# A GNN's matrix of edge counts: products of one-hots on TensorE in place of one scatter per 128 edges

## The chip, the cores and the metric

The kernel runs on one core of one Trainium2 chip. The metric is the device time of one execution in microseconds (us). Engines are named as in the profile: PE (TensorE; PEld is its weight load), DVE (VectorE), ACT (ScalarE), POOL (GpSimd) and SP (SyncE, which here only issues DMAs).

## What is computed

A graph of 6250 nodes with 128 features each and 106250 edges, sorted by destination, 17 edges a node on the mean; each node has an edge to itself. Four blocks follow one another, each as `x = layernorm(x + block(x))`:

```python
def sage(h, Wl, bl, Wr):            # block 0: two of these, with relu between
    agg = segment_sum(h[src], dst) / maximum(segment_sum(1, dst), 1)[:, None]
    return agg @ Wl.T + bl + h @ Wr.T

def gcn(x, W, b):                   # block 1: one, then relu and @ W_lin; block 2: two
    deg = segment_sum(1, dst + loops); dinv = rsqrt(deg)
    return segment_sum((x @ W)[src] * (dinv[src] * dinv[dst])[:, None], dst + loops) + b

deg = segment_sum(edge_weight, dst); dinv = where(deg > 0, rsqrt(deg), 0)   # block 3
w = dinv[src] * edge_weight * dinv[dst]
for l in range(3):                  # nine hops in all
    out = h @ W[l, 0]; x = h
    for k in range(1, 4):
        x = segment_sum(w[:, None] * x[src], dst); out = out + x @ W[l, k]
    h = relu(layernorm(h + out + bias[l]) * gamma[l] + beta[l])
```

All sums over edges are sums with the same 6250 x 6250 matrix: its entry is the number of edges from a source to a destination (blocks 0 to 2), or the sum of their weights (block 3).

## The kernel before

**Tiling.** Nodes are padded to 49 windows of 128 (`NW`). Destinations are taken in 13 chunks `c` (`NC`) of three or four windows (`SHAPE`, first window `START[c]`, width 384 or 512 columns). A product of one chunk is, for each source window `s`, a 128 x 128 table (features of 128 sources) times a 128 x 512 block of the matrix, summed in PSUM over the 49 windows `s`.

**The matrices in DRAM.** `counts` holds bytes (39 MB), `weights` holds f32 for the first eight chunks (`ND`; 100 MB). Cell (source, destination) lies in chunk order, then by source in its window (partition), source window and destination. `empty` (L203) fills them with zeros on SP's queue. The edges are cut into 49 blocks (`NB`) of 128 rows of 17 edges (`KD`). For each block

- `fetch` (L642 to L644) loads the rows' keys (destination and source in one number), records and weights by three DMAs on SP,
- `cell` (L650 to L704) works on DVE: it compares each edge with the 48 neighbours (`J`) before and behind it, so that equal edges are counted once, and makes the cell's address `celli`, its count `cval` and its weight `wval`,
- `scatter` (L575) issues 17 indirect DMAs on POOL, each writing 128 cells. All of them stand in one order, `queue`/`in_line`.

**Stage 1** is the first layer of block 0, for c = 0 to 12. `fetch_chunk(c + 2)`, a fill of `counts`, and `count_cells(c + 1)` come first, then `degrees` for the blocks of the chunk: 17 one-hots of the destinations on DVE (L718) and 17 products on PE (L719), so that the in-degree and the sum of weights come out for each node, copied by ACT (L721) and turned by PE (L724); `norms` makes the scale factors. Then `counted_sum` (from L466): every seven windows `columns` (L454) loads 448 KB of `counts` into one of seven buffers `slots`, once every scatter of the chunk's blocks is done; ACT casts two windows at a time from byte to fp32r (L488, three buffers `wides`), and PE multiplies (L495) with the high and the low half of the table, `t0hi` and `t0lo`. Where the second layer's table `t1` of the windows below `START[c]` is already there, the same cast serves a second sum, "half", which goes to DRAM (`halves`). After the sum ACT copies it out (L509), PE multiplies with the layer's weights (L428), DVE adds. After chunks 7 to 10 two "early" sums each (e = 0 to 7) take the second layer's windows from `START[e]` to 31 (`KNOWN`). A fill of 12.5 MB of `weights` is issued after each of chunks 0 to 7.

**Stage 2** is the rest of blocks 0 to 2, with the same `counted_sum`; casts alternate between DVE (`widev`) and ACT (`wides`). Beside it POOL scatters `wval` into `weights` (33 blocks, 561 DMAs), released in groups behind products by `Paced`.

**Stage 3**, the nine hops, multiplies by `weights` for the first eight chunks (L1217, loads by `columns`) and by edges gathered with indirect DMAs for the rest (L1133, L1186).

**Setup** before stage 1 loads the edges, writes `keys`, `recs` and `edges` to DRAM, checks on the chip whether the input fits this way (else `general_way` runs), and branches.

The order on each engine is the order in which the program issues (the framework adds the semaphores), so a cast, a copy or a scatter waits for all that its engine was given before it.

Of the kernel before, what the change touches and what calls it, by code (L numbers as in the profile page):

```python
# [47 lines left out]
P = 128  # L48
N = 6250
# [35 lines left out]

SLOTS, LOADS, STEP, HOTS, GROUP = 30, 12, 2, 5, 4
# [43 lines left out]
def load_weights(nc, a, const, work, ps, ident, tags):  # L130
# [18 lines left out]
    transposed("w1l", a["L0_gnn_W1l"])  # L149
    transposed("w1r", a["L0_gnn_W1r"])  # L150
    transposed("w2l", a["L0_gnn_W2l"])
    transposed("w2r", a["L0_gnn_W2r"])
    bcast("b1l", a["L0_gnn_b1l"], D)
    bcast("b2l", a["L0_gnn_b2l"], D)
# [22 lines left out]
def kernel(ctx: ExitStack, tc: tile.TileContext, a: dict, out: bass.AP):  # L177
# [15 lines left out]
    counts = dram.tile([BASE[NC] + 4 * NB * KD * P, 1], U8, name="counts")  # L193
# [6 lines left out]
    def empty(mats, dt, c, engine):  # L200
        n = 7 * width(c) // (4 if dt == U8 else 16)
        z = zeros[:].bitcast(dt)[:, :n]
        ins = fills[dt, c] = engine.dma_start(  # L203
            mats[BASE[c]:BASE[c + 1]].rearrange("(p s f) o -> p s (f o)", p=P, f=n),
            z.unsqueeze(1).to_broadcast([P, NW * width(c) // n, n])).ins
        tc.declare_no_dep(ins, group=f"cells {dt}", reason="another chunk")
        tc.add_to_no_dep_group(f"cells {dt}", ins)
        return ins

    with tc.tile_pool(name="setup", bufs=1) as setup, \  # L210
            tc.tile_pool(name="ps_setup", bufs=2, space=PSUM) as ps:

        def spread(name, ap, dt):
            t = setup.tile([P, L + 2 * J], dt, name=name)
            nc.sync.dma_start(t[:], bass.AP(ap.tensor, ap.offset, [[L, P], [1, L + 2 * J]]))
            return t
# [4 lines left out]
        dsti = spread("dsti", a["dst"], I32)  # L221
# [3 lines left out]
        main = slice(J, J + L)  # L225


# [3 lines left out]
        nc.vector.tensor_scalar(k1[:], dsti[:], 1023, 13, op0=ALU.bitwise_and, op1=ALU.logical_shift_left)  # L231
        nc.vector.tensor_scalar(k2[:], dsti[:], 20, 23, op0=ALU.logical_shift_right, op1=ALU.logical_shift_left)
# [5 lines left out]
        nc.sync.dma_start(keys[J:].rearrange("(p e) o -> p (e o)", p=P), key[:, main])  # L238


        def field(at):
# [18 lines left out]
        empty(counts, U8, 0, nc.sync)  # L260

# [7 lines left out]
        dst = setup.tile([P, L + 2 * J], F32, name="dst")  # L269
# [6 lines left out]
        nc.vector.tensor_sub(t1[:], dst[:, 2 * J:2 * J + L], dst[:, main])  # L276
        nc.vector.tensor_scalar(t2[:], dst[:, main], float(NOWHERE), None, op0=ALU.is_lt)
        nc.vector.scalar_tensor_tensor(t2[:], t1[:], 0.0, t2[:], op0=ALU.is_equal, op1=ALU.mult)
        nc.vector.tensor_reduce(odd[:, 1:2], t2[:], AX.X, ALU.max)
        nc.vector.tensor_scalar(t2[:], t1[:], float(NOWHERE // 2), None, op0=ALU.is_lt)  # L280
        nc.vector.scalar_tensor_tensor(t2[:], t1[:], 1024.0, t2[:], op0=ALU.is_ge, op1=ALU.mult)
        nc.vector.tensor_reduce(odd[:, 2:3], t2[:], AX.X, ALU.max)
# [3 lines left out]
        dmax = setup.tile([P, RPP], F32, name="dmax")  # L286
        nc.vector.tensor_reduce(dmin[:], by_row(dst[:, main]), AX.X, ALU.min)
        nc.vector.tensor_reduce(dmax[:], by_row(dst[:, main]), AX.X, ALU.max)
        rowi = setup.tile([P, RPP], I32, name="rowi")
        nc.gpsimd.iota(rowi[:], pattern=[[1, RPP]], base=0, channel_multiplier=RPP)  # L290
        nc.vector.tensor_scalar(rowi[:], rowi[:], ~(P - 1), None, op0=ALU.bitwise_and)
        even = setup.tile([P, RPP], F32, name="even")
        nc.vector.tensor_copy(even[:], rowi[:])
        d1 = setup.tile([P, RPP], F32, name="d1")
        d2 = setup.tile([P, RPP], F32, name="d2")
        nc.vector.tensor_sub(d1[:], dmax[:], even[:])
        nc.vector.tensor_scalar(d1[:], d1[:], float(2 * P), None, op0=ALU.is_ge)
# [3 lines left out]
        nc.vector.tensor_sub(d2[:], dmin[:], even[:])  # L301
        nc.vector.tensor_scalar(d2[:], d2[:], -float(P), None, op0=ALU.is_lt)
# [6 lines left out]
        row = setup.tile([P, RPP], F32, name="row")  # L309
        nc.gpsimd.iota(row[:], pattern=[[1, RPP]], base=1, channel_multiplier=RPP,  # L310
                       allow_small_or_imprecise_dtypes=True)
# [43 lines left out]
    with tc.If(go == 1) as fork:  # L355
        usual_way(tc, a, out, dram, ident, part, first, over, keys, recs, edges, counts, weights, fills, empty)
# [5 lines left out]
def usual_way(ctx, tc, a, out, dram, ident, part, first, over, keys, recs, edges, counts, weights, fills, empty):  # L362
# [9 lines left out]
    iota = const.tile([P, NEAR * P], F16, name="iota")  # L372
    nc.gpsimd.iota(iota[:], pattern=[[1, NEAR * P]], base=0, channel_multiplier=0,
# [12 lines left out]
    stacked = early.tile([P, DH], F32, name="stacked")  # L386
    nc.vector.tensor_add(stacked[:], ident[:, :DH], ident[:, DH:])
    wt = load_weights(nc, a, early, work, ps, ident, ("y", "pp"))
# [63 lines left out]
    def columns(t, c, mat, dt, step, s0):  # L452
        cw, s1 = width(c), min(s0 + step, NW)
        load = nc.sync.dma_start(t[:, :(s1 - s0) * cw], mat[BASE[c]:BASE[c + 1]].rearrange(  # L454
            "(p f) o -> p (f o)", p=P)[:, s0 * cw:s1 * cw]).ins
        needs = [ins for i in blocks_near(c) for ins in scattered[dt, i]]
        tc.declare_no_dep(load, group=f"cells {dt}", keep=needs, reason="others' cells")
        tc.add_to_no_dep_group(f"cells {dt}", load)
        for ins in needs:
            tc.add_manual_dep(load, ins.name, SYNC, reason="the matrix is complete")  # L460
        return t
# [4 lines left out]
    def counted_sum(pool, c, parts, turns, own=False, wide_bufs=3, slots=None, since=0, until=NW, also=None):  # L466
# [5 lines left out]
        for s in range(since, until):  # L472
            r = (s - since) % step
            if r == 0:
                t = next(slots) if slots is not None else pool.tile([P, step * CW], U8, name="cols", tag="cols")
                t = columns(t, c, counts, U8, min(step, until - s), s)
                if own:
                    for j, w in enumerate(windows_of(c)):
                        if s <= w < min(s + step, until):
                            loop = t[:, (w - s) * cw + j * P:(w - s) * cw + (j + 1) * P]  # L480
                            nc.vector.tensor_tensor(loop, loop, ident8[:], op=ALU.add)
            if not todo:
# [5 lines left out]
                copy(wide[:, :n * cw], t[:, r * cw:(r + n) * cw])  # L488
                todo = [wide[:, i * cw:(i + 1) * cw] for i in range(n)]
            cols = todo.pop(0)  # L490
            for into, of_block, begin, end in [(acc, parts, since, until)] + ([also] if also else []):
                if s < end:
                    lhss = of_block(s)
                    for i, lhs in enumerate(lhss):
                        product = nc.tensor.matmul(into[:, :cw], lhs, cols, start=s == begin and i == 0,  # L495
                                                   stop=s == end - 1 and i == len(lhss) - 1).ins
                paced.product(product, len(lhss))
# [16 lines left out]
    kept = ctx.enter_context(tc.tile_pool(name="kept", bufs=1))  # L514
# [53 lines left out]
    def scatter(mat, dt, vals, i):  # L568

        group = f"cells {dt}"  # L570
        needs = [fills[dt, c] for c in chunks_near(i) if (dt, c) in fills]
        mine = scattered[dt, i] = []
        bounds = {} if dt == U8 else {"bounds_check": mat.shape[0] - 1, "oob_is_err": False}
        for k in range(KD):
            ins = nc.gpsimd.indirect_dma_start(  # L575
                out=mat[:], out_offset=bass.IndirectOffsetOnAxis(ap=celli[:, i, k:k + 1], axis=0),
                in_=vals[:, i, k:k + 1], in_offset=None, **bounds).ins
            tc.declare_no_dep(ins, group=group, keep=needs, reason="no cell is written twice")
            tc.add_to_no_dep_group(group, ins)
            for need in needs:  # L580
                tc.add_manual_dep(ins, need.name, SYNC, reason="empty")
            if dt == F32:
                tc.add_manual_dep(ins, last_count.name, ORDER, reason="needed later")
            mine.append(in_line(ins))
            yield ins
        queue.append(mine[-1])

    class Paced:

        PRODUCTS, GROUP, FIRST = 3.4, 8, 80  # L590

        def __init__(self, todo):
            self.todo, self.products, self.begun = todo, 0, 0
            self.some(self.FIRST)

        def some(self, n, behind=None):
            for i in range(n):
                ins = next(self.todo, None) if self.todo else None
                if ins is not None and i == 0 and behind is not None:
                    tc.add_manual_dep(ins, behind.name, SYNC, reason="the products go ahead")  # L600

        def product(self, ins, n):
            self.products += n
            if self.todo and self.products >= self.begun * self.PRODUCTS:
                self.begun += self.GROUP
                self.some(self.GROUP, ins)

        def rest(self):
            self.some(len(dense) * KD)
            self.todo = None  # L610

    paced = Paced(None)
# [977 lines left out]
```

## Time and profile before

| | us |
|---|---|
| median of 3 runs (lowest, highest) | 5808.2 (5804.29, 5808.4) |
| the profiled execution, its own time | 5803.66 |
| its span, first to last instruction | 5801.9 |
| PE busy in the span | 5259.3 (91%) |
| POOL busy | 4159.0 (72%) |
| DVE busy | 3122.8 (54%) |
| ACT busy | 2152.6 (37%) |
| first product of stage 1 (L495) | 165.5 |
| last product of stage 1 | 1194.4 |
| first product of stage 2 | 1203.0 |
| last product of stage 2 | 2152.4 |

The mean granted clock of TensorE over the span is 0.965 of full speed. A group's line in the profile reads: line, engine, operation, output<-inputs, shapes, number; busy us and the mean ns of one; then the idle time of the engine just before these instructions and what ended most of it. "issue" means that the engine waited for nothing that the profile shows. A line of the slices has 40 digits, each the busy share of 1/40 of the span in tenths. A line of the waits reads: engine and line, what it waited for, us in total, times, longest us.

### The profile page before, as it was taken

What the parts mean: (1) busy time and instruction counts of PE and PEld (TensorE: products, weight loads), DVE (VectorE), ACT (ScalarE), POOL (GpSimd) and SP (SyncE); (2) the same over time, 40 slices, a digit from 0 to 9 for tenths busy, and PEclk for the clock granted to TensorE, in tenths of its full rate; (3) what the DMA queues carried; (4) which work ended last, traced back from release to release, by engine and by line L of the source; (5) the groups of instructions that cost most, each with busy time, mean ns of one, the idle gap of its engine ahead of it and who ended that gap; (6) DMA issues with size and microseconds to landing.
All of it is one profiled execution on the core that took longest, in us unless ns stands there. A gap on an engine that the chain in (4) does not pass through costs nothing. (4 is left out here: it accounts for less than half of the span.)

```text
span 5801.9 us, 70518 instructions
## 1 busy us (share of the span) xinstructions
PE 5259.3 (91%) x19429; PEld 3137.9 (54%) x19429; DVE 3122.8 (54%) x8865; ACT 2152.6 (37%) x4470; POOL 4159.0 (72%) x4206
## 2 busy tenths in 40 slices
PE   0657579799999999999999999999999999999997
PEld 0334457476788775555555555555455555555453
DVE  7685455258855664434446644444456544444566
ACT  1323356347655443323333323323333333333333
POOL 5777777778877417767767767767777677777776
PEclk9878799899999999999999999999999999999997
DMA  5768783146544459999999999999999999999995
GB/s 183 235 196 253 217 252 94 59 141 180 153 133 136 147 166 332 324 316 323 324 318 314 309 316 324 324 316 323 304 316 310 299 323 323 318 323 323 315 332 171
DMA packets 686931, 1503.75 MB, mean 259 GB/s; under 512 B 152167, under 2 KB 338427, under 8 KB 686267
## 3 DMA queue, kind: packets, MB, share of 16 engines
q1 hardware_dynamic: 503618, 1256.33, 64.1%
q0 software_dynamic: 134144, 182.36, 11.7%
q10 hardware_dynamic: 48760, 60.45, 3.1%
q8 instruction: 154, 2.52, 0.2%
q14 instruction: 255, 2.08, 0.1%
HBM read 1309.15 MB, written 189.54 MB: 258 GB/s over the span
## 5 line engine op out<-in xcount | busy, mean ns | idle before, releaser
L1217 PE MATMUL acc<-weighed,hop 128*128 128x512 f32 x7056 | 3380.4, 594 | 13.9 <-DMA weighed<-weights 7.5
L1133 POOL DMA_INDIRECT rows<-stored,gsrc x2763 | 2651.0, 959 | 993.6 <-issue 383.6
L1186 PE MATMUL gacc<-both,oh 128*128 128x256 f32 x2754 | 1779.0, 655 | 34.7 <-DVE both L1170 34.6
L1169 ACT ACTIVATE both<-rows,gwgt 128x128 fp32r<-128x128 f32 x2754 | 1059.7, 399 | 1979.2 <-DMA rows<-stored,gsrc 1766.8
L1217 PEld LDWEIGHTS acc<-weighed,hop 128*128 128x128 f32 x7056 | 1152.3, 190 | 938.8 <-issue 832.9
L1170 DVE SCALAR_TENSOR_TENSOR both<-rows,gwgt,both 128x128 fp32r<-128x128 f32 x2754 | 931.3, 349 | 1311.3 <-ACT both L1169 1302.2
L495 PE MATMUL acc<-wides,t 128*128 128x512 f32 (+1 forms) x3083 | 875.6, 394 | 358.3 <-ACT wides L488 237.4
L575 POOL DMA_INDIRECT counts<-cval,celli x833 | 826.3, 992 | 265.0 <-issue 243.8
L1186 PEld LDWEIGHTS gacc<-both,oh 128*128 128x128 f32 x2754 | 525.1, 191 | 691.5 <-issue 382.1
L495 PEld LDWEIGHTS acc<-wides,t 128*128 128x128 f32 x3083 | 568.3, 191 | 496.0 <-ACT wides L488 262.9
L575 POOL DMA_INDIRECT weights<-wval,celli x561 | 643.3, 1147 | 171.0 <-issue 155.5
L488 ACT CAST wides<-slots 128x1024 fp32r<-128x1024 uint8 (+3 forms) x684 | 562.5, 862 | 522.6 <-DMA slots<-counts 305.8
L1149 DVE TENSOR_TENSOR oh<-places,gdst 128x640 fp32r<-128x640 f32 x612 | 479.2, 783 | 236.3 <-PE gacc L1186 235.6
L495 PE MATMUL acc<-widev,t 128*128 128x512 f32 (+1 forms) x2044 | 575.6, 390 | 16.1 <-DVE widev L488 11.6
L495 PEld LDWEIGHTS acc<-widev,t 128*128 128x128 f32 x2044 | 376.3, 189 | 97.1 <-DVE widev L488 27.6
L718 DVE TENSOR_SCALAR oh<-iota,dloc 128x384 bf16<-128x384 f16 x833 | 215.7, 321 | 360.9 <-PE pd L719 360.7
L488 ACT CAST wides<-cols 128x1024 fp32r<-128x1024 uint8 (+1 forms) x364 | 284.7, 797 | 283.6 <-DMA cols<-counts 152.2
L488 DVE CAST widev<-cols 128x1024 fp32r<-128x1024 uint8 (+1 forms) x364 | 247.3, 684 | 175.1 <-PE acc L495 139.7
L495 PE MATMUL half<-wides,t 128*128 128x512 f32 (+1 forms) x606 | 188.3, 389 | 0.0
L719 PE MATMUL pd<-oh,lw 128*4 128x384 bf16 x833 | 176.8, 339 | 9.5 <-DVE oh L718 7.6
L488 DVE CAST widev<-slots 128x1024 fp32r<-128x1024 uint8 (+3 forms) x239 | 157.4, 676 | 17.1 <-PE acc L495 13.4
L1052 DVE TENSOR_TENSOR y<-pp,dinvw 128x256 f32<-128x256 f32 (+2 forms) x153 | 82.4, 539 | 150.1 <-PE pp L428 149.7
(266 smaller groups left out, 2792.9 us busy)
## 6 DMA issues: line engine op xcount, KB each, us to landing
weighed<-weights SPq DMA_DIRECT2D x1728, 512.0 KB
weights<-zeros SPq DMA_DIRECT2D x8, 12544.0 KB
slots<-counts SPq DMA_DIRECT2D x174, 448.0 KB
cols<-counts SPq DMA_DIRECT2D x140, 448.0 KB
rows<-stored,gsrc POOLq DMA_INDIRECT x2763
counts<-zeros SPq DMA_DIRECT2D x10, 3136.0 KB
stored<-hop ACTq DMA_DIRECT2D x74, 256.0 KB
weighed<-weights SPq DMA_DIRECT2D x72, 256.0 KB
```

The costliest lines, as they stand in the source:

```text
L488: copy(wide[:, :n * cw], t[:, r * cw:(r + n) * cw])
L495: product = nc.tensor.matmul(into[:, :cw], lhs, cols, start=s == begin and i == 0, stop=s == end - 1 and i == len(lhss) - 1).ins
L575: ins = nc.gpsimd.indirect_dma_start(out=mat[:], out_offset=bass.IndirectOffsetOnAxis(ap=celli[:, i, k:k + 1], axis=0), in_=vals[:, i, k:k ...
L718: nc.vector.tensor_scalar(oh[:], iota[:], dloc[:, k:k + 1], None, op0=ALU.is_equal)
L719: nc.tensor.matmul(acc[:], lw[:, k, :], oh[:], start=k == 0, stop=k == KD - 1)
L1052: nc.vector.tensor_tensor(y[:], po, per_node(dinvw, ws, D), op=ALU.mult)
L1133: nc.gpsimd.indirect_dma_start(out=fetched_rows[:, self.slot(self.asked), :], out_offset=None, in_=stored[self.h % 2][:], in_offset=bass.I ...
L1149: nc.vector.tensor_tensor(oh[:, :m, :], places[:].unsqueeze(1).to_broadcast([P, m, P]), gdst[:, i, ks].unsqueeze(2).to_broadcast([P, m, P] ...
L1169: nc.scalar.activation(both[:, :D], x, AF.Copy, scale=w)
L1170: nc.vector.scalar_tensor_tensor(both[:, D:], x, w, both[:, :D].bitcast(F32), op0=ALU.mult, op1=ALU.subtract)
L1186: nc.tensor.matmul(self.acc[:, j * 2 * D:(j + 1) * 2 * D], oh, both, start=k == 0, stop=k == KG - 1)
L1217: nc.tensor.matmul(acc[:, :cw], tables[h][:, s, :], t[:, s % STEP * cw:(s % STEP + 1) * cw], start=s == 0, stop=s == NW - 1)
```

## The change

Counts are no longer scattered. For four destination nodes (a group) the edges are at most 128 consecutive ones, from the row in which the first of them lies. With one edge to a partition, a one-hot of each edge's source within its window ("place", 128 columns) and a one-hot of its destination among the four and its source's window together ("zone", 4 x 49 = 196 columns) are made on DVE; place times zone on PE sums over the edges, so entry (p, (d, s)) is the count of edges from node p of window s to node d of the four. ACT copies two groups at a time from PSUM into a byte tile in which the destination is the innermost index, and the tile of one destination window (128 x 6272 bytes) goes to `counts[c]` in one DMA on SP. A window takes 32 groups: 32 products, 16 copies, four batches of eight groups on DVE.

For that:

- In the setup, `runs` (6251 rows of 256 f32) gets, for each row of 17 edges, 128 keys and 128 weights from that row on, by three DRAM to DRAM DMAs: the weights on ACT's queue, the keys on SP's in 640 and 5611 rows. `lasts` and `around` serve to find for each group the row at which its edges begin (`begin`). The check gets conditions of the new way.
- For every 128 groups (four windows) POOL gathers 128 rows of `runs` (`gathered_run`), and `prepared` splits and transposes them and makes the degrees from the same data; `degrees`, `norms`, `cval` and the fills of `counts` go. `cell` runs for the 33 blocks of `weights` only, and reads its keys from SBUF, not from a copy in PSUM.
- `building` is a generator of 784 steps (two products and a copy). 81 steps (five windows and one) are issued ahead of the first sum, and then 1.306 (4 x 16 / 49) after each source window of `counted_sum`.
- The loads of `counts` read pieces of 896 bytes for each partition and window (before: 3584), the casts read runs of 128 bytes; `wides` has two buffers, `slots` five.
- The fills of `weights` are issued in 56 parts through stage 1, and its scatters are moved from stage 2 into stage 1: three blocks after each chunk. `Paced` goes. A part of the layers' weights is loaded at the start of stage 2.

The core of the diff:

```diff
+        nc.scalar.dma_start(runs[:, RUN:], bass.AP(a["edge_weight"].tensor, a["edge_weight"].offset + J,
+                                                    [[KD, N + 1], [1, RUN]]))
...
         nc.sync.dma_start(keys[J:].rearrange("(p e) o -> p (e o)", p=P), key[:, main])
+        for r in (slice(0, 5 * P), slice(5 * P, N + 1)):
+            nc.sync.dma_start(runs[r, :RUN], bass.AP(keys.tensor, keys.offset + J + r.start * KD,
+                                                     [[KD, r.stop - r.start], [1, RUN]]))
...
+    def count_columns(t, c, step, s0):
+        n = SHAPE[c]
+        t = t[:, :n * step * P].rearrange("p (w s f) -> p w s f", s=step, f=P)
+        nc.sync.dma_start(t.rearrange("p w s f -> p w (s f)"), counts[c].rearrange(
+            "(w p f) o -> p w (f o)", w=n, p=P)[:, :, s0 * P:(s0 + step) * P])
+        return t
...
-                copy(wide[:, :n * cw], t[:, r * cw:(r + n) * cw])
+                copy(wide[:, :n * cw].rearrange("p (s w f) -> p s w f", s=n, f=P),
+                     t[:, :, r:r + n, :].rearrange("p w s f -> p s w f"))
...
+            if meanwhile is not None:
+                meanwhile()
...
-        def degrees(i):
...
+        def gathered_run(b):
+            t = cells.tile([P, 2 * RUN], F32, name="run", bufs=3)
+            ins = nc.gpsimd.indirect_dma_start(
+                out=t[:], out_offset=None, in_=runs[:],
+                in_offset=bass.IndirectOffsetOnAxis(ap=begin[:, b:b + 1], axis=0)).ins
+            queue.append(in_line(ins))
+            return t
...
+        def hot(name, places, spots, k0, n):
+            t = hots.tile([P, SOME // 2, n, 2], BF16, name=name)
+            nc.vector.tensor_tensor(
+                t[:], places[:].unsqueeze(1).to_broadcast([P, SOME // 2, n, 2]),
+                spots[:, k0:k0 + SOME].rearrange("p (j o) -> p j o", o=2).unsqueeze(2).to_broadcast(
+                    [P, SOME // 2, n, 2]), op=ALU.is_equal)
+            return t
...
+        def building():
...
+            for w in range(NW):
+                b, c = w // WPB, chunk_of(w)
+                if w % WPB == 0:
+                    if b + 1 < NBATCH:
+                        found[b + 1] = gathered_run(b + 1)
+                    spots[b] = prepared(b, found.pop(b))
+                t = spare if w % 2 else cells.tile([P, NW * P], U8, name="built")[:]
+                by_column = t.rearrange("p (s f) -> p f s", f=P)
+                for some in range(GROUPS_W // SOME):
+                    k0 = w % WPB * GROUPS_W + some * SOME
+                    zone = hot("zone", zones2, spots[b], k0, NZ)
+                    place = hot("place", places2, spots[b], P + k0, P)
+                    for pair in range(SOME // 2):
+                        acc = ps_build.tile([P, 2, CW // 2], F32, name="some")
+                        for i in range(2):
+                            nc.tensor.matmul(acc[:, i, :NZ], place[:, pair, :, i], zone[:, pair, :, i],
+                                             start=True, stop=True)
+                        f = some * SOME * G + pair * 2 * G
+                        nc.scalar.copy(by_column[:, f:f + 2 * G, :].rearrange("p (i d) s -> p i d s", d=G),
+                                       acc[:, :, :NZ].rearrange("p i (d s) -> p i d s", s=NW))
+                        yield
+                nc.sync.dma_start(counts[c].rearrange("(w p f) o -> w p (f o)", w=SHAPE[c], p=P)[w - START[c]], t)
...
+        meanwhile.add(building(), 4 * PAIRS_W / NW)
+        meanwhile.some(0, 5 * PAIRS_W + 1)
...
+        meanwhile.add(filling, ND * FILLS / (NW * 10))
...
         for c in range(NC):
             n, ws = of(c)
-            fetch_chunk(c + 2)
-            if c + 4 < NC:
-                empty(counts, U8, c + 4, nc.sync)
-            count_cells(c + 1)
-            for i in sorted(i for i in blocks_near(c) if i in degs):
-                degrees(i)
-            norms(c)
...
+            for i in dense[PER * c:PER * (c + 1)]:
+                filled(chunks_near(i))
+                cell(i, fetch(i))
+        meanwhile.rest()
...
-    last_count = queue[-1]
-    paced = Paced(ins for i in dense for ins in scatter(weights, F32, wval, i))
```

In this, P is 128, G is 4, SOME is 8, and `zones2`, `places2` hold the numbers that the one-hots compare with. The instructions issued on PE go from 15129 to 16594, on DVE from 9842 to 9573, on ACT from 4552 to 5021.

## The prediction, made before the changed kernel was timed

> **What bounds the kernel now.** I began with the slices of the page.
>
> ```profile
> PE   0657579799999999999999999999999999999997
> POOL 5777777778877417767767767767777677777776
> PEclk9878799899999999999999999999999999999997
> ```
>
> One slice is 145 us. From slice 9 on PE is at 90% or more; only the first eight slices (up to about 1190 us) leave room on it. The busy times by stretch say the same with sums: columns are PE, PEld, DVE, ACT, POOL busy us (instructions), then clock, DMA share, GB/s.
>
> ```profile
> 34.00:165.00 131.00, 1.84 (x4) 0.72 (x4) 75.85 (x270) 8.16 (x19) 91.76 (x93) 1.00 0.50 149
> 165.00:1195.00 1030.00, 751.90 (x3502) 521.63 (x3503) 545.38 (x2106) 437.51 (x584) 787.40 (x797) 0.86 0.60 183
> 1195.00:1500.00 305.00, 278.70 (x1368) 217.88 (x1367) 252.25 (x663) 188.20 (x287) 243.13 (x204) 0.97 0.63 181
> 1500.00:2152.00 652.00, 641.65 (x3050) 531.10 (x3049) 415.88 (x957) 340.94 (x473) 384.38 (x341) 1.00 0.49 139
> 2152.00:5802.00 3650.00, 3584.14 (x11508) 1865.96 (x11506) 1805.99 (x4817) 1169.89 (x3102) 2651.01 (x2763) 0.99 0.92 313
> ```
>
> The hops after 2152 us and stage 2 (1195 to 2152) are PE at 98%. The edit touches what ends at 1195: PE is busy 752 of 1030 us there and starts only at 165. The waits from 150 to 1150 us name who makes it late:
>
> ```profile
> DVE oh L718 <- PE pd L719: 360.7, 38, 65.7
> ACT wides L488 <- DMA slots<-counts: 305.8, 10, 91.5
> POOL counts L575 <- issue: 221.0, 725, 0.3
> PE acc L495 <- DMA slots<-counts: 120.8, 1, 120.8
> ```
>
> ACT's casts wait ten times for a load of counts, and a load waits for its chunk's scatters. The scatters, seen alone in stretches of 100 us:
>
> ```profile
> 600.00:700.00 100.00, 76.23 (x79) 0.76 0.73 224
> 800.00:900.00 100.00, 76.25 (x78) 1.00 0.78 240
> 1100.00:1200.00 100.00, 76.25 (x78) 0.93 0.18 51
> ```
>
> 75 to 79 of them per 100 us from 100 to 1150 us, one every 1.27 us, the rest of that time "issue": POOL never pauses. From 46.8 us, 833 counts scatters take until 1105 us; the last chunk's products end at 1194. So **the counts scatters on POOL pace stage 1**.
>
> **The change part by part.** Prices come from these groups (busy us, mean ns):
>
> ```profile
> L575 POOL DMA_INDIRECT counts<-cval,celli x833 | 826.3, 992 | 265.0 <-issue 243.8 <-DVE wval L699 11.7 <-DMA counts<-cval,celli 4.0
> L488 ACT CAST wides<-slots 128x1024 fp32r<-128x1024 uint8 x270 | 269.8, 1044 | 381.3 <-DMA slots<-counts 305.8 <-PE half L495 58.2 <-PE acc L495 7.7
> L718 DVE TENSOR_SCALAR oh<-iota,dloc 128x384 bf16<-128x384 f16 x833 | 215.7, 321 | 360.9 <-PE pd L719 360.7
> L666 DVE TENSOR_TENSOR before<-m,aside 128x816 bf16<-128x816 f32 x49 | 48.7, 993 | 0.0
> L721 ACT COPY degT<-pd 4x384 f32<-4x384 f32 x49 | 22.9, 468 | 160.0 <-PE pd L719 146.5 <-DVE oh L718 12.3 <-DMA slots<-counts 1.2
> L263 ACT CAST edge<-dsti 128x850 f32<-128x850 int32 x1 | 1.4, 1358 | 0.0
> L257 ACT CAST rec<-s 128x850 f32<-128x850 int32 x1 | 0.9, 907 | 0.8 <-DVE s L256 0.8
> ```
>
> *Removed.* 833 scatters, 833 one-hots (216 us DVE), 833 products pd (177 us PE), 49 degT (23 us ACT), 16 blocks' cells, 39 MB of fills. With them goes POOL's pace. What is late next: the counts now come from DVE (one-hots), PE (1568 products of 196 columns) and ACT (784 evictions).
>
> *The eviction, e us each.* 392 elements from PSUM, written as bytes 128 bytes apart. No row has that step. Contiguous: casts of 1024 and 512 elements (1044 and 617 ns) give 0.83 ns an element, started 0.95 us apart for 1024; L721's 384 from PSUM took 468 ns, some 0.1 of it overlapped by the next. That makes e = 0.39, the low end. L263 writes every 12 bytes: such casts start 1.21 us apart, runs like L257's 0.84, so 1.31 ns an element, or e = 0.57. The step here is ten times wider again. I take twice the contiguous price, 1.66 ns: 392 x 1.66 + 0.07 = **0.72**; one more increment of L263's size, 1.79 ns, makes 0.77, my high end. L263 is nearest in kind, but its step still puts neighbours close, hence my choice above it.
>
> The Trainium skill, "SBUF — State Buffer", says that memory is reached in lines of 16 bytes and that fewer than two elements in a line cost rate. L263, with 1.33 elements in a line, is slower as that says. By the rule an element here has a line to itself, some two ACT cycles each, and the sum would stay near the forecast; by L263's row alone it would be rival 1's.
>
> *One-hots on DVE.* A batch of eight groups compares 1568 + 1024 elements and feeds four evictions: 196 batches. L666's two-input form: 993 ns for 816, and 685 for 512 elements (L556), so 1.01 ns an element and 0.17 fixed: 2.96 us a batch, the high end. L718's 16-bit form: (321 - 166)/384 = 0.40 ns: 1.37 us, the low end. All operands are 16-bit, so nearest L718: 1.5.
>
> *The new start.* Before any build, `runs` must be filled. 6251 rows of weights go first on ACT's queue; `keys` waits for that copy's semaphore lane, the two copies of keys (640 and 5611 rows) for `keys`, and gather 0 and the setup of the places on POOL for both copies and for `edges`, queued behind them on SP. Price: a 512-byte packet took 27 ns in the trace. How many of 16 engines share it? The 106 rows of `x` (75.75 to 77.21 us) ran as two streams, 24 ns apart in each, although others were free; 106 = 2 x 53. 6251 = 7 x 893 so takes 893 x 28 ns = 25 us; 5611 = 31 x 181 has no divisor up to 16 but 1, so all rows run on one engine, 157 us. On 16 it would be 10; at 50 ns a packet (both ends of a copy, untested) 280. I take 157: keys land near 32 us, copies at 193, first eviction near 205 (a gather, then about ten small DVE operations, 7 us).
>
> The skill's "DMA: Bandwidth & Descriptors", on why a DMA counts 16, gives just this rule: the largest k up to 16 that divides the slow dimensions. The trace's 106 rows agree. By it the sum is the forecast; were it not to hold for a DRAM copy, 147 us less (rival 2).
>
> *Then 82 evictions* stand ahead of the first cast in ACT's order: 82 e = 59 us. First product near **264** (165 before).
>
> *Build section.* The other 702 evictions are spread over 545 of the stage's 781 steps. ACT: 273 casts x 0.96 = 262, chunk ends 36, 702 x 0.72 = 505: 803 us. DVE: 175 batches x 1.5 = 262, preparing 77, cells 28 x 6 = 170, chunk ends 47: 556 (at 2.96: 812). PE: 285 products, 141 builds, 45 other: 471. ACT bounds it; for handing over between three engines I add 4%, an estimate (a well-fed PE was busy 98.4% and 99.6% of 800 to 900 and 1600 to 1700): 1.04 x 803 = 835.
>
> *POOL beside it.* 561 weights scatters move here, 51 a chunk, with the gathers of batches 4 and later queued behind them. At 1.27 us that is 65 us a chunk, under ACT's 92 (835 over nine); fills of weights in 56 parts on SP share its queue with loads. Nothing added.
>
> *Tail.* 236 steps with 790 products and no builds: before, 378 products per 100 us (800 to 900), so 209; less since many are 384 wide: 195. Casts there (118 x 0.96) fit beside it.
>
> *Stage 2* loses the scatters beside DVE's casts but was PE-bound at 98%; its loads have packets of 896 bytes (41 ns against 140 for 3584, so 1.31 against 1.12 us a load on each engine, behind spare buffers). 0 to -15: I take -8. The hops are untouched; weights are complete long before 2152 in both kernels, so nothing: the cover is over 800 us.
>
> Sum: stage 1 ends at 205 + 82e + 1.04(298 + 702e) + 195 = 710 + 812e, against 1195; with stage 2, **change = 812e - 493**. e = 0.72 gives +92. On the profiled execution's 5803.66 us (span 5801.9; the runs' median, 5808.2, is 0.08% above) that is **5895**.
>
> **Rivals.**
> 1. *The strided write is cheaper.* Break-even is e = 0.61. At L263's price, 0.57: -30, 5773. At the contiguous price, 0.39: -176, 5627 (DVE's 556 x 1.04 still under ACT's 572 x 1.04). For: only one row speaks for a stride. Against: that row is dearer for each element. This is the other side, decided by one duration.
> 2. *The 5611 rows run on 16 engines.* 147 us off: 5748 at e = 0.72. For: DRAM copies of such rows are not in the trace. Against: the 106 rows.
> 3. *The change does not take POOL's pace away, or DVE's takes its place.* In stage 2, beside DVE's casts, 68 scatters fit 100 us (1300 to 1400), 1.46 us each: 74 a chunk, still covered. At 1.9 us, 97 a chunk: gathers late, 5 x 9 = 45 us, and a last batch stalls more: up to +190 over stage 1. Or one-hots at 2.96: 812 beside ACT's 803, each stalling the other, 10% instead of 4%: 50 us. Packets at 50 ns: +123. So 5940 to 6080.
>
> **How the numbers follow.** Forecast (5870 to 5935): 0.37. Rival 1: 0.36, a half at each price. Rival 2: 0.10. Rival 3: 0.17. A measurement of this kernel can tell about 0.2%, or 12 us, from no change; of the cases around break-even I give 0.06 to that (0.04 from rival 1, 0.02 from the forecast). Faster: 0.32 + 0.10 = 0.42; slower: 0.35 + 0.17 = 0.52. The range, 5635 to 6020, leaves out the lowest of rival 1 (0.10) and the top of rival 3 (0.07). The forecast's own range is 5870 to 5935.
>
> **What would show it.** First product at 264; copies of keys landing near 193, with one DMA engine busy meanwhile; 784 evictions at 0.72 us start to start; ACT over 90% busy from 264 to 1100 and PE near 56%; POOL idle between scatters; last build near 1100; stage 2 as long as before. Wrong if evictions take under 0.6, if the runs copies land before 60 us, or if ACT waits for DVE or for gathers.

## The result, and the profile after

The changed kernel takes 6675.4 us (median of 4 runs, 6672.6 to 6678.8) against 5808.3 (5804.3 to 5811.1): 1.1496 times the time before, 95% interval 1.1482 to 1.151, **867 us slower**. The prediction had 5895 and a range up to 6020; the direction was as forecast, the amount nine times the 92 us of the forecast. (Five of the experiments below ran on two chips where the kernel before itself took 7878 and 7788 us; their stages and whole times are not compared with those of the others, and two of the five were run again.)

The slices of the changed kernel, one of 167 us each:

```profile
PE   0256666666689999999999999999999999999997
...
ACT  0899999999974665543333333232333333333333
POOL 0033333423540000016767777676777767777776
PEclk9955555565589999999999999999999999999998
```

POOL's pace is gone, as intended: from the third slice to the end of stage 1 it is mostly at 20% to 60%. ACT has taken its place, at 90% or more in the third to the eleventh slice, and PE waits with it. The stretches (PE, PEld, DVE, ACT, POOL busy, clock, DMA share, GB/s):

```profile
200.00:400.00 200.00, 77.74 (x272) 42.97 (x272) 61.95 (x114) 198.28 (x130) 0.00 (x0) 0.90 0.33 104
400.00:800.00 400.00, 248.59 (x810) 151.27 (x810) 149.49 (x316) 394.13 (x284) 168.44 (x156) 0.56 0.42 126
...
1890.00:2085.00 195.00, 181.45 (x863) 147.46 (x862) 19.39 (x40) 117.29 (x148) 39.66 (x40) 1.00 0.32 89
2100.00:3028.00 928.00, 894.67 (x4383) 740.08 (x4382) 647.60 (x1610) 524.73 (x756) 33.23 (x33) 1.00 0.55 152
3032.00:6676.00 3644.00, 3575.89 (x11496) 1860.37 (x11496) 1813.74 (x4816) 1181.59 (x3101) 2651.46 (x2763) 0.99 0.92 313
```

ACT is busy 381 to 394 of every 400 us while it has evictions, from 200 to 1884 us. When they end (1890 to 2085), PE is at once at 93%. The hops are what they were (3644 us from 3032 on, before 3650). So all of the loss lies before 2085: the last product of stage 1 ends at 2085 instead of 1194, 890 us later, and stage 2 gives 22 us back (first to last product 928 us, before 949). The groups of stage 1, by shape (busy us, mean ns, idle before them):

```profile
L838 ACT CAST built<-some 128x392 uint8<-128x392 f32 x400 | 770.9, 2318 | 0.0
L838 ACT CAST slots<-some 128x392 uint8<-128x392 f32 x384 | 730.4, 2298 | 3.0 <-PE some L835 3.0
...
L531 ACT CAST wides<-slots 128x1024 fp32r<-128x1024 uint8 x236 | 334.4, 1425 | 29.2 <-PE half L539 23.4 <-PE acc L539 3.4 <-issue 1.7
...
L799 DVE TENSOR_TENSOR zone<-zones,spots 128x1568 bf16<-128x1568 bf16 x196 | 190.9, 974 | 804.5 <-PE some L835 804.4
...
L799 DVE TENSOR_TENSOR place<-places,spots 128x1024 bf16<-128x1024 bf16 x196 | 133.9, 683 | 0.0
```

L838 is the eviction, under the name of either tile that it fills: 784 of them, ACT hardly idle before one (3 us in all). The mean of 2.3 us overlaps the next; three in a row show the distance of two starts (start, us):

```profile
600.39 1.56 ACT L531 CAST wides<-slots 128x1024 fp32r<-128x1024 uint8 x1
601.64 3.90 ACT L838 CAST built<-some 128x392 uint8<-128x392 f32 x2
604.82 1.14 ACT L531 CAST wides<-slots 128x512 fp32r<-128x512 uint8 x1
...
607.06 5.99 ACT L838 CAST built<-some 128x392 uint8<-128x392 f32 x3
612.31 1.16 ACT L554 COPY agg<-acc 128x512 f32<-128x512 f32 x1
```

Three starts in 612.31 - 607.06 = 5.25 us: **1.75 us an eviction**, where the prediction had 0.72. Beside a cast the time is only shared out otherwise: the cast at 600.39 is followed after 1.25 us instead of 0.95, and the two evictions behind it after 3.18 us instead of 3.5, so the three take 4.43 us, as 0.95 + 2 x 1.75 = 4.45. The waits from 200 to 2000 us tell the same from the other side:

```profile
DVE zone L799 <- PE some L835: 804.4, 167, 10.4
POOL weights L617 <- DVE low L724: 559.6, 10, 179.6
PE some L835 <- ACT built L838: 311.8, 356, 3.1
PE some L835 <- ACT slots L838: 293.5, 323, 2.1
```

DVE's one-hots wait for PE, PE for ACT, POOL for DVE's cells, and ACT for hardly anyone.

### The profile page after: what moved, and what is told of

Same layout as the page of the kernel before. It is cut to its first block, busy times and chain, and to the rows that moved or that the text cites. A ratio compares the mean times of both kernels' runs of the same rounds, so it can differ in the third digit from the quotient of the medians.

```text
span 6676.5 us, 70849 instructions
## 1 busy us (share of the span) xinstructions
PE 5685.6 (85%) x20147; PEld 3384.9 (51%) x20147; DVE 3137.6 (47%) x7899; ACT 3494.0 (52%) x5205; POOL 3310.2 (50%) x3395
## 4 chain that ended last, share of the span: by engine, by line
PE 45%; ACT 24%; DMA 18%; issue 5%; DVE 4%; another core or an unknown queue 2%; POOL 2%; ACTq 0%; POOLq 0%; SPq 0%; DVEq 0%
PE acc L1333 27%; DMA rows<-stored,gsrc 16%; PE acc L539 10%; ACT built L838 9%; ACT slots L838 9%; ACT wides L531 4%; PE gacc L1302 3%; PE pp L460 2%; POOL rows L1249 2%; DMA cols<-counts 1%; PE half L539 1%; DVE both L1286 1%; ACT both L1285 1%; DVE widev L531 1%
## 5 line engine op out<-in xcount | busy, mean ns | idle before, releaser
L539 PE MATMUL acc<-wides,t 128*128 128x512 f32 (+1 forms) x3083 | 1181.7, 479 | 55.3 <-ACT wides L531 55.2
L617 POOL DMA_INDIRECT weights<-wval,celli x561 | 604.2, 1077 | 1133.3 <-DVE low L724 559.6
L835 PE MATMUL some<-zone,place 128*128 128x196 bf16 x1568 | 367.1, 334 | 625.7 <-ACT built L838 311.8
L531 ACT CAST wides<-slots 128x1024 fp32r<-128x1024 uint8 (+3 forms) x684 | 722.8, 1072 | 177.1 <-PE half L539 88.2
L838 ACT CAST built<-some 128x392 uint8<-128x392 f32 x400 | 770.9, 2318 | 0.0
L539 PEld LDWEIGHTS acc<-wides,t 128*128 128x128 f32 x3083 | 659.6, 228 | 212.8 <-ACT wides L531 141.2
L838 ACT CAST slots<-some 128x392 uint8<-128x392 f32 x384 | 730.4, 2298 | 3.0 <-PE some L835 3.0
L835 PEld LDWEIGHTS <-place 128*128 128x128 bf16 x1568 | 188.0, 123 | 914.2 <-issue 898.1
L799 DVE TENSOR_TENSOR zone<-zones,spots 128x1568 bf16<-128x1568 bf16 x196 | 190.9, 974 | 804.5 <-PE some L835 804.4
L973 POOL DMA_INDIRECT gm<-recs,gat x17 | 17.5, 1027 | 876.6 <-DVE gwgt L990 873.6
```

The costliest lines, as they stand in the source:

```text
L531: copy(wide[:, :n * cw].rearrange("p (s w f) -> p s w f", s=n, f=P), t[:, :, r:r + n, :].rearrange("p w s f -> p s w f"))
L617: ins = nc.gpsimd.indirect_dma_start(out=weights[:], out_offset=bass.IndirectOffsetOnAxis(ap=celli[:, i, k:k + 1], axis=0), in_=wval[:, i, ...
L799: nc.vector.tensor_tensor(t[:], places[:].unsqueeze(1).to_broadcast([P, SOME // 2, n, 2]), spots[:, k0:k0 + SOME].rearrange("p (j o) -> p ...
L835: nc.tensor.matmul(acc[:, i, :NZ], place[:, pair, :, i], zone[:, pair, :, i], start=True, stop=True)
L838: nc.scalar.copy(by_column[:, f:f + 2 * G, :].rearrange("p (i d) s -> p i d s", d=G), acc[:, :, :NZ].rearrange("p i (d s) -> p i d s", s=NW))
```

## The experiments

Theory: single bytes written 128 bytes apart make the eviction slow, and the eviction is the time. Rivals: the conversion to bytes, the read from PSUM, other engines in the way; and, for the time, another limit right behind the eviction.

### The eviction by itself

A kernel with nothing but forms of this copy, eight of each (REPS), one execution; `source()` is the eviction's 392 elements, from PSUM except where the tile's name says `flat`, which lies in SBUF:

```diff
+            o = t.rearrange("p (s f) -> p f s", f=step)[:, :8, :].rearrange("p (i d) s -> p i d s", d=4)
+        for r in range(REPS):
+            copy(o, source())
```

> Leaves out the whole computation: each form of copy runs eight times with nothing beside it, and the output is zeros. In the changed kernel one eviction (392 elements from PSUM, bytes written 128 bytes apart) starts 1.75 us after the one before. Theory S, the step of the written bytes: 1.75 us here too, about 0.4 for the same bytes in a run, and DVE's copy is slow as well. Theory B, the conversion of f32 to bytes: 1.75 at every step, and 0.4 to 0.6 for f32 written at the same step. Theory M, the read from PSUM in two pieces of 196: 1.75 for a run of bytes too, 0.4 from SBUF. Theory C, other engines and DMAs in the way: 0.4 to 0.7 for all forms here. Also measured: the same eight bytes of a place as runs of 4, 8, 16 and 32, and the cast of 1024 bytes read in pieces of 128 (0.95 if the pieces cost nothing).

The groups of that kernel; the tile's name tells the engine and the form, "kernel" being a step of 128 bytes (mean ns of one, eight in "busy"):

```profile
L46 ACT CAST act_byte_sbuf<-flat 128x392 uint8<-128x392 f32 x8 | 15.5, 1932 | 5.8 <-SPq L35 5.6
L46 POOL CAST pool_byte_kernel<-flat 128x392 uint8<-128x392 f32 x8 | 15.4, 1927 | 0.6 <-SPq L35 0.2
L46 ACT CAST act_byte_kernel<-acc 128x392 uint8<-128x392 f32 x8 | 15.2, 1900 | 5.8 <-SPq L35 5.6
L46 ACT CAST act_half_kernel<-acc 128x392 bf16<-128x392 f32 x8 | 15.2, 1899 | 3.2 <-SPq L35 2.9
L46 DVE CAST dve_byte_kernel<-acc 128x392 uint8<-128x392 f32 x8 | 15.2, 1899 | 5.8 <-SPq L35 5.6
L46 ACT CAST act_byte_sixteen<-acc 128x392 uint8<-128x392 f32 x8 | 15.1, 1892 | 1.2 <-SPq L35 1.0
...
L46 ACT CAST act_byte_eight<-acc 128x392 uint8<-128x392 f32 x8 | 8.3, 1042 | 0.9 <-SPq L35 0.7
...
L46 ACT COPY act_float_kernel<-acc 128x392 f32<-128x392 f32 x8 | 6.5, 812 | 1.9 <-SPq L35 1.6
...
L46 DVE CAST dve_byte_runs<-acc 128x392 uint8<-128x392 f32 x8 | 4.5, 566 | 182.3 <-SPq L35 182.0
L46 ACT CAST act_byte_runs<-acc 128x392 uint8<-128x392 f32 x8 | 3.9, 485 | 0.2
L46 ACT COPY act_float_runs<-acc 128x392 f32<-128x392 f32 x8 | 3.9, 485 | 0.9 <-SPq L35 0.7
L79 ACT CAST act_runs_of_eight<-acc 128x392 uint8<-128x392 f32 x8 | 3.9, 485 | 53.8 <-SPq L35 53.6
L92 ACT CAST act_runs_of_four<-acc 128x392 uint8<-128x392 f32 x8 | 3.9, 485 | 29.8 <-SPq L35 29.6
```

At the step of the change: 1.90 us. The same bytes in one run: 0.485. So not the conversion, and not PSUM (from SBUF 1.93); nothing ran beside it, so not other engines. Theory S holds for ACT and for DVE (0.566 for the bytes in one run). POOL took 1.93 at this step too, but was not tried with a run. The other rows say more. The step need not be 128: at 16 bytes it is 1.89, at 8 bytes 1.04. Four-byte words at a step of 128 bytes take 0.81 (0.485 in one run), but two-byte ones 1.90 again. And four bytes side by side, then the next four 128 bytes on, are as cheap as one run. So a place of one or two bytes, 16 bytes or more from the next, is dear, and four bytes side by side are enough to avoid it. Why, the rows leave open: counted by places, the runs of four take 485 / 98 = 4.9 ns a place, no less than the single bytes (1900 / 392 = 4.8), so it may be the number of places that costs, for bytes and two-byte words, and not what is written at each. Casts that read pieces of 128 bytes took 1045 ns, as in one piece.

### Evictions written in a run

```diff
-                by_column = t.rearrange("p (s f) -> p f s", f=P)
+                by_column = t.rearrange("p (f s) -> p f s", s=NW)
```

> The changed kernel with the same 784 evictions written as runs (392 consecutive bytes), so that the counts lie in another order than the casts read them; all else is as it was. Theory S: an eviction every 0.39 us as long as PE and DVE follow; the prediction's sum 710 + 812 x 0.39 gives a stage 1 of 1027 us, but DVE's batch measured 1.66 us and not 1.5 (175 x 0.16 = 28 us more), so DVE bounds it: about 1050, some 5650 in all. Theories B, M and C: still 1.75 us, 6675.

7091.6 us, against 7878.0 for the kernel before on the same chip. An eviction took 0.52 us (mean of 784), which speaks for S; the expected 5650 and the length of stage 1 can't be tested there.

### Runs of eight bytes

The same counts in the same places, but the zone's columns have the source window first, so that one copy can write the eight destinations of a place side by side:

```diff
-        nc.gpsimd.iota(zones2.rearrange("p (d s) o -> p d s o", s=NW), pattern=[[64, G], [1, NW], [0, 2]], base=0,
+        nc.gpsimd.iota(zones2.rearrange("p (s d) o -> p s d o", d=G), pattern=[[1, NW], [64, G], [0, 2]], base=0,
...
-                        nc.scalar.copy(by_column[:, f:f + 2 * G, :].rearrange("p (i d) s -> p i d s", d=G),
-                                       acc[:, :, :NZ].rearrange("p i (d s) -> p i d s", s=NW))
+                        nc.scalar.copy(by_source[:, :, f:f + 2 * G].rearrange("p s (i d) -> p s i d", d=G),
+                                       acc[:, :, :NZ].rearrange("p i (s d) -> p s i d", d=G))
```

> The changed kernel with the zone's columns ordered source window first, so that an eviction writes runs of 8 bytes; the counts land in the same places. Alone, such an eviction took 0.485 us against 1.9 at the step of the change. Theory (the step of single bytes is what made the change slow): sum 710 + 812 x 0.485 = 1104 us for stage 1, where ACT (298 + 702 x 0.485 = 638) and DVE (584 with batches of 1.66 us) are close, so up to 60 us more for their coupling; stage 2 as long as in the changed kernel, 29 us shorter than before: 5680 to 5750 in all, faster than before. Rival (the write step is one limit of two, and PE at its low granted clock, or the wait of POOL for cells, takes over): stage 1 over 1250, 5830 or more.

5992.2 us, 1.0318 (1.0301 to 1.0336) of the kernel before: 683 us of the 867 went with the single bytes. But the expectation, 5750 at most, missed by 240. The last product of stage 1 is at 1401, not at 1104 to 1164, and ACT is busy only 103 of 200 us (600 to 800). The waits from 220 to 1450 us:

```profile
DVE ki L747 <- DMA run<-runs,begin: 318.4, 8, 47.0
PEld L835 <- DVE place L799: 281.3, 20, 47.0
PE some L835 <- DVE place L799: 272.9, 14, 46.7
ACT built L838 <- PE some L835: 240.6, 39, 46.6
POOL weights L617 <- DVE low L724: 201.4, 5, 76.9
```

The first line is the new one: eight times DVE waits some 40 us for the gathered rows of a batch, and PE and ACT wait in a chain behind it. In the changed kernel this wait was 45.5 us in all. The rival is right, another limit right behind, and it begins with the second of its guesses: POOL waits for cells (201 us in the last line), and what the gathers behind it lose is handed on to DVE. POOL's own order shows it, here from one gather to the next:

```profile
649.56 0.99 POOL L735 DMA_INDIRECT run<-runs,begin  x1 [0.30 <-issue]
685.23 1.71 POOL L617 DMA_INDIRECT weights<-wval,celli  x1 [34.68 <-DVE low L724]
...
755.09 0.99 POOL L735 DMA_INDIRECT run<-runs,begin  x1 [0.30 <-issue]
```

Between the two stand 51 scatters: POOL waits 34.68 us for the first one's cells, then works for 70 us, and only then issues the gather that DVE is waiting for.

### Evictions on two engines

```diff
-                        nc.scalar.copy(by_column[:, f:f + 2 * G, :].rearrange("p (i d) s -> p i d s", d=G),
+                        (nc.scalar.copy if pair % 2 else nc.vector.tensor_copy)(by_column[:, f:f + 2 * G, :].rearrange("p (i d) s -> p i d s", d=G),
```

> The changed kernel with its strided evictions taken in turn by ACT and DVE. Alone each engine took 1.9 us for one. Theory W (each engine waits for its own write): ACT then has 298 + 351 x 1.75 = 912, DVE 584 + 351 x 1.75 = 1198 us in the build section, and DVE bounds it: stage 1 ends near 205 + 72 + 1.04 x 1198 + 195 = 1718 against 2085, 6310 in all. Rival X (the two engines share what makes the write slow): evictions of both get longer than 2.5 us while both write, and stage 1 stays near 2085.

6300.0 us, 1.0848 (1.0826 to 1.087), 6310 by theory W; the last product of stage 1 is at 1701 (1718 by W). The evictions' groups:

```profile
L838 ACT CAST built<-some 128x392 uint8<-128x392 f32 x200 | 394.6, 1973 | 134.8 <-PE some L835 134.0
L838 DVE CAST built<-some 128x392 uint8<-128x392 f32 x200 | 392.9, 1965 | 33.7 <-PE some L835 30.4 <-issue 1.7
```

Both take 1.97 us side by side, 1.90 alone: the engines do not share what makes the write slow. X falls.

### The copies into `runs`

> The changed kernel with the copies into runs cut into 6240 + 11 rows of weights and 640 + 5600 + 11 rows of keys; 6240, 640 and 5600 are multiples of 16. Theory: 5611 = 31 x 181 put all rows on one DMA engine, 136 us from 33 to 169 us. Then the first eviction is at 60 to 75 us and not 200.7, and the time is 125 to 140 us shorter, about 6540. Rival, the copies are slow for another reason (short rows, or DRAM to DRAM): the first eviction stays at 200 and the time at 6675.

```diff
-        nc.scalar.dma_start(runs[:, RUN:], bass.AP(a["edge_weight"].tensor, a["edge_weight"].offset + J,
-                                                    [[KD, N + 1], [1, RUN]]))
+        for r in (slice(0, 6240), slice(6240, N + 1)):
+            nc.scalar.dma_start(runs[r, RUN:], bass.AP(a["edge_weight"].tensor, a["edge_weight"].offset + J + r.start * KD,
+                                                       [[KD, r.stop - r.start], [1, RUN]]))
...
-        for r in (slice(0, 5 * P), slice(5 * P, N + 1)):
+        for r in (slice(0, 5 * P), slice(5 * P, 6240), slice(6240, N + 1)):
```

In the changed kernel, the DMA that follows the 5611 rows on SP is held for 135 us (timeline: start, us):

```profile
31.48 1.38 SPq L268 DMA_DIRECT2D runs<-keys  x2
32.96 135.35 SPq L307 DMA_DIRECT2D edges<-edge  x1
```

The cut copies alone took 7661.9 us, beside 7878.0 of the kernel before; the changed kernel was not run on that chip, so the gain in time is open there. The first eviction was at 83.1 us, behind the 60 to 75 expected, where the changed kernel has it at 200.7. Together with the runs of eight, on a chip where the kernel before took 5809:

> As runs_of_eight, and the copies into runs in rows that 16 divides. Theory: the first eviction at 70 instead of 200 us, and nothing else is in the way then: 125 to 135 us less than runs_of_eight, 5550 to 5620. Rival (POOL's 561 weights scatters or the fills of weights become late once the start is early): less than 60 us gained.

5876.0 us, 1.0117 (1.01 to 1.0134): 116 less than with the runs of eight alone. The DMA behind the copies is no longer held:

```profile
33.13 0.42 SPq L308 DMA_DIRECT2D edges<-edge  x1
```

The first eviction is at 78.4, 122 us earlier. The theory holds, with a gain a little under its 125 to 135; the 5550 to 5620 that it gave for the whole missed by 256, since it was counted from the expectation for the runs of eight, which had missed. DVE's wait for gathers stays (331 us).

### Gathers ahead

```diff
-            t = cells.tile([P, 2 * RUN], F32, name="run", bufs=3)
+            t = cells.tile([P, 2 * RUN], F32, name="run", bufs=6)
...
-            found[0] = gathered_run(0)
+            for b in range(5):
+                found[b] = gathered_run(b)
...
-                    if b + 1 < NBATCH:
-                        found[b + 1] = gathered_run(b + 1)
+                    if b + 5 < NBATCH:
+                        found[b + 5] = gathered_run(b + 5)
```

> runs_of_eight with the gathers of runs issued five batches ahead (six buffers instead of three), so that they stand on POOL before scatters that they followed. In runs_of_eight DVE waited 318 us for gathers in eight places. Theory (a gather is late because it is queued on POOL behind weights scatters, and these wait in turn for cells that DVE makes between its batches): that wait is under 40 us, the last product of stage 1 is at 1090 to 1160 instead of 1401, and the time is 240 to 310 us less than runs_of_eight, 5680 to 5750. Rival (scatters or fills slow the gather itself, or the weights scatters only move the wait to another place): less than 100 us gained.

> All three repairs: runs of 8 bytes, copies in rows that 16 divides, gathers five batches ahead. Theory: the gains add, so the last product of stage 1 is at 970 to 1040, and the time 5570 to 5640, faster than the kernel before. Rival (POOL with 561 scatters, over 700 us of work in 1000, becomes the bound): the last scatter ends after the last product of stage 1, and the time stays above 5680.

Both ran on the chip where the kernel before took 7788 (6997.1 and 6858.6 beside 7788.4) and settle nothing; the same two kernels again:

> The same kernel as gathers_ahead, in the hope of a chip whose memory nobody else uses (the first was measured beside a kernel before of 7788 us). Theory (gathers queued behind scatters): DVE's wait for gathers under 40 us, last product of stage 1 at 1090 to 1160, 5680 to 5750. Rival (the wait moves to another place): above 5890.

5679.0 us, 0.9774 (0.9753 to 0.9795). The last product of stage 1 is at 1085.6, and DVE waits for gathers for 4.6 us in all, where it was 323. The wait did not move elsewhere.

> The same kernel as gathers_ahead_copies_on_16. Theory (the three gains add): last product of stage 1 at 970 to 1040, 5570 to 5640. Rival (POOL's scatters become the bound): above 5680, and the last scatter behind the last product of stage 1.

**5566.2 us, 0.9581 (0.9564 to 0.9598)**: 245 us faster than the kernel before beside it (5811.0), 1109 faster than the change as it was made. The gains add: 683 + 313 + 116 = 1112. Both expectations are undercut by a little: the last product of stage 1 is at 969.6 (970 to 1040), the time under 5570. Its slices:

```profile
PE   3888989999999999999999999999999999999997
...
ACT  4888985476554433233333233233333233233333
POOL 1688887200000277677677677677677677777776
PEclk9999999999999999999999999999999999999997
```

PE is at 80% or more from the second slice on, and no engine stands still in stage 1. POOL's last scatter starts at 1017, 47 us behind the last product of stage 1; half of the rival is so, but stage 2 does not wait for it.

### The kernel before on the chip of these runs

> The kernel before, unchanged, on the same chip as the other three, so that stages can be compared: 5808 if the chip is like that of the first profile, with hops of 3650 us after 2152.

5810.7 us, ratio 1.0003 (0.9993 to 1.0013), first product at 160, last one of stage 1 at 1198, for comparison with runs_of_eight and its companions.

## Why the prediction was wrong, point by point

- *POOL's scatters pace stage 1*: borne out. With them gone, and the three faults repaired, stage 1 ends 225 us earlier than in the kernel before. (The last counts scatter starts at 1126, not at 1105.)
- *The eviction, e = 0.72, 0.77 at most*: **this step failed**. It measured 1.75 us in place and 1.90 alone. In the prediction's own sum that is 812 x (1.75 - 0.72) = 836 us, and the forecast missed by 780. The prediction reasoned from L263, the dearest strided write of the trace, and took its step for what mattered; but L263 writes four-byte words. For words of four bytes the reasoning was nearly right (0.81 measured at the step of 128 bytes). That single bytes cost 2.3 times as much again, no row of the trace showed; the "high end" was a choice and no bound, and there the range broke. Rival 1, a cheaper write, lay on the other side. The sign came out as forecast because the write was dear at all; the size came from a price for another width.
- *The sum*: right in form while ACT is the limit. 710 + 812 x 1.75 = 2131 us for stage 1; 2085 measured. ACT idled for 36 of the 1490 us from 400 to 1890, so the 4% for handing over was too much; without it the sum is 2070. With cheap evictions it holds only once the gathers are repaired: at 0.485, the price alone, it gives 1104, and at 0.38, the distance of two starts in place (two evictions from 395.73 to 396.49 us of gathers_ahead_2), 1019; runs_of_eight measured 1401 and gathers_ahead_2 1086.
- *The Trainium skill, "SBUF — State Buffer", Specifications, its lines of 16 bytes*: the rule spoke against this write, and the rows agree in direction: steps of 16 and 128 bytes cost the same (1.89 and 1.90), a step of 8 about half. The two cycles that the prediction made of it are a price the rows show for four-byte words only.
- *The start*: right in its cause, and partly by luck in its number. First eviction predicted at 205, measured 200.7. The 5611 rows cost 135 us (157 predicted), and from the end of that to the first eviction it was 32 us instead of 12; the two errors cancel. Cut into rows that 16 divides the copies no longer hold the next DMA, and the first eviction is 122 us earlier. So the rule of the Trainium skill, "DMA: Bandwidth & Descriptors", on why a DMA counts 16, held for these DRAM copies, and rival 2 falls. (The 106 rows of `x` lie at 65 to 66.6 us, counted like all other times here, and not at 75.75 to 77.21; their length is as the prediction read it.) The first product, 264 predicted, came at 346.5: 82 evictions at 1.75.
- *One-hots on DVE at 1.5 us a batch*: 0.974 + 0.683 = 1.66 measured; nearly right.
- *POOL beside it, nothing added*: wrong, and hidden by the eviction. The prediction counted 51 scatters at 1.27 us against a chunk and found 65 under 92. It left out that a scatter waits for its cell, that DVE makes cells only where they stand among its batches, and that a gather queued behind such scatters holds up the next batch. With the cheap evictions that is 318 us of DVE's time; rival 3 had the place, but sought the cause in the scatter's price, which in the stretch shown is 70 / 51 = 1.37 us instead of 1.27.
- *Stage 2, -8*: -22 measured. PE's idle time in it is the same (32 us before, 33 after); it is PE's busy time that fell, from 917 to 895 us, with a granted clock of 0.99 and 1.00. The scatters beside DVE's casts are gone too (casts of 128x1024 from `cols` 719 ns before, 693 after). The cause was not tried. (PE was busy 96% of 1195 to 2152 in the kernel before, 91% of its first 305 us, and not 98%.)

## What to carry to other kernels

When a new operation decides the sum and no row of the trace has its form, the nearest row is no bound: ask what else differs, the width of what is written as well as the step, and leave the range open there. Order the indices of a product so that a copy out of PSUM writes at least four bytes side by side; here, with eight, that was one pattern, worth 683 us. On a queue in order, count what each entry waits for, not only how long it takes: a gather behind scatters is as late as the cells of those scatters.

## What the runs showed of the hardware

- Copies of 392 elements (evictions_alone), the fixed part of the instruction included: one or two bytes at a place of its own, 128 bytes from the next, took 4.8 ns (1.90 us / 392) on ACT, and bytes the same on DVE; four bytes 2.1 ns; bytes in runs of four or more 1.2 ns each.
- A cast of 1024 elements behind such an eviction started 1.25 us ahead of its successor instead of 0.95, and the eviction behind the cast gave the time back: the sum of the three rows at 600.39 us is what their prices apart give.
- Rows of 512 bytes from DRAM to DRAM took some 24 ns each (135 us / 5611) where the number of rows had no divisor up to 16 but 1; the 6251 = 7 x 893 rows of weights, whose packets lie from 4.7 to 27.4 us of the changed kernel's trace, took 3.6 ns each, about a seventh.
- The granted clock was 0.54 to 0.59 between 400 and 1890 us of the changed kernel, where PE was busy some 63%, against 0.97 to 1.00 in stage 1 of the last version, at 86% to 91%. The busy share alone does not set it: from 600 to 800 us runs_of_eight had 0.79 with PE busy 55%, the changed kernel 0.59 with 63%. There the changed kernel's products waited for evictions 77 times, 0.9 us each, and those of runs_of_eight for DVE twice, some 40 us each; what decides was not tried. Products of 512 columns took 642 ns on the mean in the changed kernel's first 2000 us, against 414 in the kernel before up to 1190. PE was waiting for ACT all the same.
